# Two-layer kernel: softmax division moved behind the weighted values, and the values' projection by seven half-size products

## The chip, the core and the metric

The kernel runs on one core of a Trainium2 chip. The metric is the device time of one execution in microseconds (us). Times of single instructions come from one profiled execution. The core's engines run side by side, each through its own queue in order: TensorE (PE; PEld is its weight load), VectorE (DVE), ScalarE (ACT), GpSimd (POOL) and SyncE (SP), which here only issues DMA transfers. Matrix products land in eight PSUM banks of 128 partitions x 512 floats.

## The reference

The input x is 8 batch elements of 512 tokens of 256 channels, float32. Two layers follow one another; layer 1 of the change's title is the first. It normalises x, and adds causal attention with 16 heads of 64 channels (with biases and rotary embedding) and an int8-quantised linear map:

```python
xn = layernorm(x)
q, k, v = xn @ Wq + bq, xn @ Wk + bk, xn @ Wv + bv      # 1024 columns: 16 heads of 64
q, k = rope(q), rope(k)
scores = where(causal, q @ k.T / sqrt(64), -1e9)
attended = softmax(scores) @ v                            # per head
x = x + (attended @ Wo + bo) + quantised_linear(xn)
```

The second layer normalises again and adds a gated comparison softmax and a token-mixing feed-forward block. The change touches nothing in it.

## The kernel before

**Steps.** The first layer is worked through in 16 steps, called `at`: step `at = 2b + g` is half g (8 heads) of batch element b. A step's order is written out by hand in the loop `for at in range(1, last)` (`last` is 15); steps 0 and 15 are written out before and behind it. Each engine's queue takes its instructions in the order in which the functions are called.

**Projections.** `project_qk(n, which)` (L428, L434) projects q (`which` 0) or k (1) of four heads: two halves of two matmuls 128x512, each evicted from PSUM by ACT with its bias into `l`; then four DMAs (L436) put `l` with its partitions exchanged into `y`. `turn_qk` does the rotary embedding: on DVE `h = l*cos` (`turn_own`, L446) and `y = y*sin` (`turn_other`, L446), on POOL `h = h + y` (L461). Step `at` uses the heads of projections `2at` and `2at+1`; they are made one step earlier. `project_v(at)` (L472, L478, L479) makes the values of the next step with eight matmuls of 128x512 columns; ACT evicts them, a DMA stores them to HBM, and `load_v` (L489) brings them back with their partitions in another order. A matmul in float32 is two records in the profile.

**Scores.** `scores(at, run)` (L509) computes, for five runs of query blocks of 32, the scores of all heads side by side on the array. `soften` follows each run: DVE adds the mask and finds the row maximum (L537), and ACT takes the exponential and sums it (L541). `divide` takes the reciprocal of the sums on DVE (L552) and multiplies every probability by it on POOL (L560; in step 0 some on ACT, L558). `turn` transposes 32x32 blocks on DVE (L580). `weigh` (L597) multiplies with the values on TensorE, `keep_weighed` (L611) evicts four banks on ACT and adds the values' bias. `finish` is the output product with Wo (`output_product`, L390) and its addition to x on DVE (`add_output`, L399), which frees the product's bank.

**The input.** `look_at` takes the statistics of a batch element and lets POOL raise them to the power -1/2 (L158); `prepare` normalises it on DVE (L172) and finds its greatest magnitude (L306). `turn_x` transposes it on DVE into a tile `xs` (L325), stores it (`xnf`, L329) and loads it back as `xnT` (L188), which the projections read. In the last steps `fetch_input` also loads the first elements' normalised input again as `xnl`, which shares its tile with `xs`; `round_input` (L192), `clip` (L197, L201) and `add_quantised` (L209 to L218) do the quantised map.

**Order of a step before.** In the words of the functions: scores(at, 0), turn(at-1, 4), soften; weigh(at-1), keep_weighed(at-1); rotary of the next keys; scores 1, soften, turn 0, divide; `project(at+1, 0)`, the next queries; scores 2, soften, rotary, turn 1; turn_x in even steps; `project_v(at+1)`; scores 3 and 4 with their soften, turn and divide; `finish(at-1)`; `project(at+2, 1)`, the keys of the step after the next. Tiles of PSUM come from a ring of eight banks: a new tile waits until the one eight tiles earlier has been read.

Of the kernel before, what the change touches and what calls it, by code (L numbers as in the profile page):

```python
# [16 lines left out]
P = 128  # L17
B, S, D = 8, 512, 256
H, L = 16, 64
NT = S // P  # L20
# [14 lines left out]
PLACE = {i: n for n, i in enumerate(i for us in UNITS for i in us)}  # L35
# [9 lines left out]
def two_layers(  # L45
# [214 lines left out]
    with ExitStack() as c0:  # L260
# [120 lines left out]

        products = {}

        def output_product(at, half):

            pw = bank(f"pw_{at}_{half}").rearrange("p (j n) -> p j n", j=2)
            for j in range(2):
                tok = bass.ts(2 * half + j, P)
                for p in range(4):
                    nc.tensor.matmul(  # L390
                        pw[:, j, :], atts[at, p][:, tok], wo[:, 4 * (at % NH) + p, :],
                        start=(p == 0), stop=(p == 3),
                    )
            products[at, half] = pw
# [20 lines left out]
        def project_qk(at, which):  # L415


            b, g = divmod(at, NG)
            w = wqkv[which]

            l, y = (
                prob.tile([P, 2, S], F32, tag="p", name=f"{tag}_{at}_{which}") if at == 1 else
                work.tile([P, 2, S], F32, tag=tag, name=f"{tag}_{at}_{which}", bufs=2) for tag in "ly"
            )
            for t in range(2):
                pb = bank(f"pq_{at}_{which}_{t}")
                for k in range(NK):
                    nc.tensor.matmul(  # L428
                        pb.rearrange("p (t a r) -> p t a r", a=4, r=Q), w[:, g, k, bass.ts(t, P)],
                        xnT[b][:, k].rearrange("p a (t r) -> p t a r", r=Q),  # L430
                        start=(k == 0), stop=(k == NK - 1),
                    )
                bias = BIAS + which * NP + 2 * g + t
                nc.scalar.activation(l[:, t, :], pb, AF.Identity, bias=cs[:, bias : bias + 1])  # L434
            for n in range(4):
                nc.sync.dma_start(y[bass.ts(n ^ 1, Q)], l[bass.ts(n, Q)])  # L436
            evicted[at, which] = l, y
# [45 lines left out]

        def load_v(at):

            there = stores.pop(at)
            vs[at] = work.tile([P, 4, NT, P], F32, tag="vr", name=f"vr_{at}")
            for j in range(4):
                nc.sync.dma_start(  # L489
                    vs[at][j * Q : j * Q + Q].rearrange("p c t n -> p c (t n)"),  # L490
                    there[j].rearrange("(c k) n -> k c n", c=4),
                )
# [23 lines left out]
        def soften(at, run):  # L516

            if at not in sums_of:
                sums_of[at] = [
                    small.tile([P, 2 * len(PLACE)], F32, tag=f"{n}16", name=f"{n}_{at}", bufs=2)  # L520
                    for n in ("nm", "sm", "rs")
                ]
            nm, sm, _ = sums_of[at]
            for us in RUNS[run]:
# [7 lines left out]
                for i in us:  # L532
                    n = Q * (i + 1)
                    chances[at, i] = p[:, :, col : col + n]
                    for e, sc in enumerate(scored.pop((at, i))):
                        c = 2 * PLACE[i] + e
                        nc.vector.tensor_tensor_reduce(  # L537
                            p[:, e, col : col + n], sc, cmask[:, S - n :], -1.0 / L**0.5, BIG,
                            ALU.add, ALU.min, nm[:, c : c + 1],
                        )  # L540
                        nc.scalar.activation(  # L541
                            p[:, e, col : col + n], p[:, e, col : col + n], AF.Exp,
                            bias=nm[:, c : c + 1], scale=-1.0, accum_out=sm[:, c : c + 1],
                        )
                    col += n

        def divide(at, run, on_act=False):
            _, sm, rs = sums_of[at]
            for us in RUNS[run]:
                first = 2 * PLACE[us[0]]  # L550
                which = slice(first, first + 2 * len(us))
                nc.vector.reciprocal(rs[:, which], sm[:, which])  # L552
                for i in us:
                    for e in range(2):
                        c = 2 * PLACE[i] + e
                        p = chances[at, i][:, e, :]
                        if on_act and us is RUNS[run][-1]:
                            nc.scalar.activation(p, p, AF.Copy, scale=rs[:, c : c + 1])  # L558
                        else:
                            nc.gpsimd.tensor_scalar(p, p, rs[:, c : c + 1], 1.0, ALU.mult, ALU.mult)  # L560

# [4 lines left out]
        def turn(at, run):  # L568
# [6 lines left out]
            for i in (i for us in RUNS[run] for i in us):  # L575
# [29 lines left out]
        def keep_weighed(at):  # L605
            g = at % NH
            for j, av in enumerate(weighed.pop(at)):
                atts[at, j] = attp.tile([P, S], F32, tag="att", name=f"att_{at}_{j}")

                bv = BIAS + 2 * NP + 4 * g + j  # L610
                nc.scalar.activation(atts[at, j], av, AF.Identity, bias=cs[:, bv : bv + 1])  # L611
# [200 lines left out]
        divide(0, 0)  # L812
# [4 lines left out]
        divide(0, 1, on_act=True)  # L817
# [8 lines left out]
        divide(0, 2)  # L826
# [9 lines left out]
        divide(0, 3, on_act=True)  # L836
        divide(0, 4)
# [4 lines left out]
        for at in range(1, last):  # L842
# [5 lines left out]
            turn(at - 1, 4)  # L848
# [15 lines left out]
            divide(at, 0)  # L864
            turn_qk(2 * at + 3, 1)
            if at == last - 2:
                first_norm = norm(0, xpool.tile([P, NT, D], F32, tag="x", name="yn_0"))
# [8 lines left out]
            elif g == 1 and 1 <= b < B - 2:  # L876
                look_at(b + 2)
            divide(at, 1)
            if at == last - 1:
                first_norm()  # L880
            project(at + 1, 0)
            if at in (last - 3, last - 2):
# [8 lines left out]
            divide(at, 2)  # L891
            if at == 2:
                prepare(2)
            elif g == 1 and 1 <= b < B - 2:
                prepare(b + 2)
            if g == 0 and 1 < b < B - 1:
                turn_x(b + 1)
                if b + 2 < B:
                    x_next.append(load_x(b + 2))
            if at == last - 1:  # L900
                turn_qk(2 * at + 3, 0)
            if at == 1:
                nc.gpsimd.tensor_tensor(bob, bob, rw[:, 2, :], ALU.add)
                add_biases(0)
            project_v(at + 1)
            if at == last - 1:
                break
            if at == 2:
# [3 lines left out]
            soften(at, 3)  # L912
            turn_qk(2 * at + 3, 0)
            turn(at, 2)
            divide(at, 3)
            scores(at, 4)
            soften(at, 4)
# [3 lines left out]
            finish(at - 1)  # L921
            turn(at, 3)
            if two:
                project(at + 2, 1)
            divide(at, 4)
# [11 lines left out]
        divide(at - 1, 3)  # L937
# [6 lines left out]
        divide(at - 1, 4)  # L944
# [5 lines left out]
        turn(at - 1, 4)  # L950
        add_output(at - 2, 1)
        fetch(B - 1)
        divide(at, 0)
# [6 lines left out]
        divide(at, 1)  # L960
        keep_weighed(at - 1)
        load_v(at)
# [7 lines left out]
        divide(at, 2)  # L970
# [5 lines left out]
        divide(at, 3)  # L976
# [5 lines left out]
        divide(at, 4)  # L982
        kk = key(0)
        turn(at, 4)
        r = gate(0)
# [124 lines left out]
```

## Time and profile before

| What | Value |
|---|---|
| Time, median of 3 runs | 935.56 us (935.55 to 936.3) |
| Profiled execution: span from first to last instruction | 934.3 us; its own time outside the trace is not listed apart, the runs lie 1.3 us above the span |
| PE busy | 919.8 us (98%) |
| PEld, DVE, ACT, POOL busy | 594.7, 793.3, 528.3, 542.2 us |
| Granted TensorE clock | 1.000 |
| First layer's steps on the chain (starts of scores 0, steps 2 to 14) | 115.93, 163.36, 207.59, 253.73, 297.96, 342.94, 387.18, 431.68, 475.92, 521.62, 565.85, 612.07, 657.00 us |
| L472, values' projection | 256 records of 128x512, 114.3 us |
| L390, output product | 512 records of 128x256, 114.9 us |
| L560, divides on POOL | 504, 265.4 us |
| L552, reciprocals on DVE | 144, 15.7 us |
| DMA | 108.03 MB, 116 GB/s over the span |

The page's group rows give an engine, an operation, its output and inputs by the program's names, the shape, the count, and then busy time, mean ns of one, and the idle time of the engine just before, with what ended it. The chain that ended last is followed back from the last instruction, at each step to what released it.

### The profile page before, as it was taken

How to read it: one execution, taken by the hardware profiler on the slowest of the kernel's cores; microseconds unless marked ns; L12 is line 12 of the kernel's file. 1: busy time of each engine (PE TensorE's matmuls, PEld its weight loads, DVE VectorE, ACT ScalarE, POOL GpSimd, SP SyncE). 2: the span in 40 equal slices, each digit the busy share in tenths (PEclk: the TensorE clock that was granted, in tenths of full speed). 3: DMA queues.
4: the chain of work that ended last, by engine and by line, in shares of the span. 5: the costliest groups of instructions: out<-in, count | busy, mean ns of one | idle time of the engine just before them, and what ended most of it. 6: DMA issues, size and time to landing. Idle time of an engine off the chain costs nothing.

```text
span 934.3 us, 27432 instructions
## 1 busy us (share of the span) xinstructions
PE 919.8 (98%) x10451; PEld 594.7 (64%) x10451; DVE 793.3 (85%) x2441; ACT 528.3 (57%) x1478; POOL 542.2 (58%) x688
## 2 busy tenths in 40 slices
PE   9998999999999999999999999999999999999998
PEld 5446565656566575757565656566657777777776
DVE  4998898898899889988998899999899588888854
ACT  3585564647465646474746556555577444445553
POOL 2576766655665667566665756678667323444311
PEclk9999999999999999999999999999999999999999
DMA  7667354525543464245444635563435133221011
GB/s 213 194 165 213 102 138 130 121 75 132 169 105 97 109 182 132 75 115 172 123 95 114 179 93 145 151 154 97 110 108 127 47 102 79 74 50 48 25 33 34
DMA packets 70290, 108.03 MB, mean 116 GB/s; under 512 B 8592, under 2 KB 49040, under 8 KB 70160
## 3 DMA queue, kind: packets, MB, share of 16 engines
q1 hardware_dynamic: 68288, 104.64, 42.2%
q10 hardware_dynamic: 1872, 1.64, 0.7%
q8 instruction: 83, 1.36, 0.6%
q14 instruction: 47, 0.39, 0.1%
HBM read 41.76 MB, written 28.84 MB: 76 GB/s over the span
## 4 chain that ended last, share of the span: by engine, by line
PE 85%; DVE 6%; DMA 3%; issue 1%; POOL 1%; SPq 1%; ACT 1%; DVEq 0%; ACTq 0%; POOLq 0%
PE pq L428 21%; PE av L597 14%; PE sc L509 11%; PE pw L390 10%; PE pv L472 8%; PE po L756 6%; PE pk L703 3%; PE pg L718 3%; PE pvv L730 3%; DVE t L580 2%; PE c L675 2%; PE trc L743 1%; PE plr L245 1%; DVE p L537 1%; DMA xnl<-xnf 1%
## 5 line engine op out<-in xcount | busy, mean ns | idle before, releaser
L541 ACT ACTIVATE p<-p,nm 128x64 f32<-128x64 f32 (+15 forms) x512 | 260.0, 512 | 123.8 <-DVE nm L537 100.9
L560 POOL TENSOR_SCALAR p<-p,rs 128x512 f32<-128x512 f32 (+4 forms) x504 | 265.4, 547 | 44.6 <-DVE rs L552 42.6
L461 POOL TENSOR_TENSOR h<-h,y 128x1024 f32<-128x1024 f32 x62 | 161.1, 2598 | 181.5 <-DVE y L446 102.2
L537 DVE CUSTOM_DVE_ANT_0 p<-sc,cmask 128x64 f32<-128x64 f32 (+15 forms) x512 | 190.2, 434 | 53.7 <-PE sc L509 53.7
L580 DVE STREAM_TRANSPOSE t<-p 128x256 f32<-128x256 f32 (+3 forms) x640 | 192.2, 367 | 17.9 <-POOL p L560 17.8
L509 PE MATMUL sc<-h,h 64*32 64x512 f32 (+15 forms) x4096 | 138.7, 393 | 1.3 <-POOL h L461 1.2
L597 PE MATMUL av<-t,vr 32*64 32x384 f32 (+15 forms) x4096 | 128.8, 392 | 3.7 <-issue 3.7
L597 PEld LDWEIGHTS av<-t,vr 32*64 32x64 f32 x4096 | 122.8, 131 | 9.2 <-issue 7.9
L509 PEld LDWEIGHTS sc<-h,h 64*32 64x32 f32 x4096 | 78.6, 106 | 78.5 <-issue 58.3
L434 ACT ACTIVATE l<-pq,cs 128x512 f32<-128x512 f32 x128 | 84.7, 683 | 67.6 <-PE pq L428 53.3
L390 PE MATMUL pw<-wo,att 128*128 128x256 f32 x512 | 114.9, 382 | 0.8 <-DVE nm L537 0.8
L446 DVE TENSOR_TENSOR y<-y,cs 128x1024 f32<-128x1024 f32 x64 | 110.6, 1728 | 5.1 <-DMA y<-l 5.1
L428 PE MATMUL pq<-xnT,wq 128*128 128x512 f32 x256 | 114.6, 599 | 0.2 <-ACT xnT L349 0.2
L428 PE MATMUL pq<-xnT,wk 128*128 128x512 f32 x256 | 113.1, 593 | 1.4 <-DVE x L399 1.0
L472 PE MATMUL pv<-wv,xnT 128*128 128x512 f32 x256 | 114.3, 599 | 0.0
L390 PEld LDWEIGHTS pw<-wo,att 128*128 128x128 f32 x512 | 95.9, 190 | 19.5 <-issue 6.1
L541 ACT ACTIVATION_READ_ACCUMULATOR p<-p,nm 128x1 f32 x512 | 97.3, 190 | 0.0
L428 PEld LDWEIGHTS pq<-xnT,wk 128*128 128x128 f32 x256 | 48.3, 190 | 58.2 <-issue 55.4
L472 PEld LDWEIGHTS pv<-wv,xnT 128*128 128x128 f32 x256 | 47.3, 190 | 57.9 <-issue 54.5
L446 DVE TENSOR_TENSOR h<-l,cs 128x1024 f32<-128x1024 f32 x64 | 80.0, 1252 | 4.3 <-ACT l L434 4.3
L428 PEld LDWEIGHTS pq<-xnT,wq 128*128 128x128 f32 x256 | 47.2, 190 | 56.0 <-issue 48.8
L611 ACT ACTIVATE att<-av,cs 128x512 f32<-128x512 f32 x64 | 38.7, 688 | 71.3 <-PE av L597 71.3
(114 smaller groups left out, 940.7 us busy)
## 6 DMA issues: line engine op xcount, KB each, us to landing
y<-l SPq DMA_DIRECT2D x256, 128.0 KB, 2.3
va<-v SPq DMA_DIRECT2D x32, 512.0 KB, 3.1
vr<-va SPq DMA_DIRECT2D x64, 256.0 KB, 5.1
x<-in_x SPq DMA_DIRECT2D x15, 512.0 KB, 5.0
x1f<-x SPq DMA_DIRECT2D x7, 512.0 KB, 3.2
out<-y SPq DMA_DIRECT2D x14, 256.0 KB, 2.2
xnf<-xs SPq DMA_DIRECT2D x5, 512.0 KB, 3.6
xnT<-xnf SPq DMA_DIRECT2D x20, 128.0 KB, 2.8
```

Of the source, the lines that this page charges most:

```text
L390: nc.tensor.matmul(pw[:, j, :], atts[at, p][:, tok], wo[:, 4 * (at % NH) + p, :], start=(p == 0), stop=(p == 3),)
L428: nc.tensor.matmul(pb.rearrange("p (t a r) -> p t a r", a=4, r=Q), w[:, g, k, bass.ts(t, P)], xnT[b][:, k].rearrange("p a (t r) -> p t a r ...
L434: nc.scalar.activation(l[:, t, :], pb, AF.Identity, bias=cs[:, bias : bias + 1])
L446: nc.vector.tensor_tensor(dst, src, table[:, None, :].to_broadcast([P, 2, S]), ALU.mult)
L461: (engine or nc.gpsimd).tensor_tensor(h, h, y, ALU.add)
L472: nc.tensor.matmul(pb.rearrange("p (g n) -> p g n", g=2), xnT[b][:, k, 2 * half + j], wqkv[2][:, 2 * g : 2 * g + 2, k, :], start=(k == 0), ...
L509: nc.tensor.matmul(scored[at, i][e][j * Q : j * Q + Q, :], q[rows, j % 2, bass.ts(i, Q)], k[rows, j % 2, :n], start=True, stop=True,)
L537: nc.vector.tensor_tensor_reduce(p[:, e, col : col + n], sc, cmask[:, S - n :], -1.0 / L**0.5, BIG, ALU.add, ALU.min, nm[:, c : c + 1],)
L541: nc.scalar.activation(p[:, e, col : col + n], p[:, e, col : col + n], AF.Exp, bias=nm[:, c : c + 1], scale=-1.0, accum_out=sm[:, c : c + 1],)
L560: nc.gpsimd.tensor_scalar(p, p, rs[:, c : c + 1], 1.0, ALU.mult, ALU.mult)
L580: nc.vector.transpose(turned[at][c][:, :, at_ : at_ + (n - 1) * pitch(c) + 1 : pitch(c), :], p[:, :, c * P : c * P + n * Q].rearrange("p e ...
L597: nc.tensor.matmul(banks[j][e * L : e * L + L, i * Q :], vs[at][rows, c, m, bass.ts(e, L)], t[c][rows, e, m * pitch(c) + m : m * pitch(c) ...
```

## The change

Three things are changed, and the hand-written order of a step with them.

First, `divide` is gone. `weigh` works on the exponentials; `settle` takes the reciprocals of all sums of a step at once, transposes them on DVE, writes them to HBM and loads them back spread over the partitions (`share`), and `share_out` multiplies the weighted values by them on POOL (in step 15 two of four on DVE). The values' bias no longer goes through `keep_weighed`: since probabilities sum to one, `gather_bias` and `spread_bias` put its product with Wo once into the output's bias row. `soften` is split into `lower` (DVE) and `raise_` (ACT).

Second, in steps 1 to 14 `project_v(at+1)` is replaced by `project_v_by_seven(at+1)`: seven products of half the size in place of eight (Winograd's form), with differences of the input's quarters made on POOL (`mix_input`, once per batch element), sums of the weights made once on POOL (`sum_weights`), and the results put together by accumulation in PSUM, four ACT copies and three DVE additions. Its products stand among the halves of the keys' projections; in step 14 they stand alone.

Third, moved: `finish(at-1)` from the end of the step to the place where `project_v` stood; `turn_x` of steps 4, 6, 8, 10 in front of the queries' projection, and `look_at` and `prepare` in odd steps to an earlier place; `turn_x` of step 12 stays behind `clip`; the rotary embedding of the step's last queries goes behind `lower(at, 4)`.

```diff
+        def mix_input(b):
+            t = work.tile([P, 4, 2, P], F32, tag="tx", name=f"tx_{b}")
+            (b11, b12), (b21, b22) = ([xnT[b][:, k, 2 * h : 2 * h + 2] for h in range(2)] for k in range(NK))
+            for dst, x, y in ((0, b12, b11), (1, b22, t[:, 0]), (2, b22, b12), (3, b21, t[:, 1])):
+                nc.gpsimd.tensor_tensor(t[:, dst], x, y, ALU.subtract)
...
+        def project_v_by_seven(at, amid={}):
...
+            x, y, z = (bank(f"pv_{at}_{n}").rearrange("p (j n) -> p j n", j=2) for n in range(3))
...
+            product(x, b11, a11, True)
+            keep(0, 0)
+            then(0)
+            product(y, b21, a12, True)
+            product(z, t1, s1, True)
+            product(x, t2, s2)
+            keep(1, 0)
+            add(y, 0, 0)
+            then(1)
+            product(x, t3, s3)
+            keep(1, 1)
+            then(2)
+            add(z, 1, 1)
+            product(x, t4, a22)
+            keep(0, 1)
+            store(0)
+            then(3)
+            product(z, b22, s4)
+            add(z, 1, 0)
+            store(1)
...
-        def divide(at, run, on_act=False):
...
+        def settle(at):
+            sm = sums_of.pop(at)[1]
...
+            nc.vector.reciprocal(rs, sm)
+            nc.vector.transpose(turned_, rs)
+            there = away.tile([4, 2, S], F32, tag="rs", name=f"rsf_{at}")
+            nc.sync.dma_start(there.rearrange("j e (i q) -> (j e i) q", q=Q), turned_)
+            shares[at] = work.tile([P, 4, S], F32, tag="share", name=f"share_{at}")
+            for e in range(2):
+                nc.sync.dma_start(
+                    shares[at][e * L : e * L + L], there[:, e, :][None].to_broadcast([L, 4, S])
+                )
...
+        def share_out(at, j):
+            nc.gpsimd.tensor_tensor(atts[at, j], atts[at, j], shares[at][:, j, :], ALU.mult)
...
             scores(at, 0)
-            turn(at - 1, 4)
+            if at == 1:
+                turn(at - 1, 4)
+                settle(at - 1)
             soften(at, 0)
...
-            divide(at, 0)
             turn_qk(2 * at + 3, 1)
+            for j in range(4):
+                share_out(at - 1, j)
+            if g == 1 and 1 <= b < B - 2:
+                look_at(b + 2)
...
             elif g == 1 and 1 <= b < B - 2:
-                look_at(b + 2)
-            divide(at, 1)
+                prepare(b + 2)
+            if g == 0 and 1 < b < B - 2:
+                turn_x(b + 1)
+                x_next.append(load_x(b + 2))
...
             project(at + 1, 0)
+            if at == 1:
+                sum_weights()
+            if g == 1:
+                mix_input(b + 1)
...
-            divide(at, 2)
+            if at == last - 3:
+                turn_x(b + 1)
...
-            if g == 0 and 1 < b < B - 1:
-                turn_x(b + 1)
-                if b + 2 < B:
-                    x_next.append(load_x(b + 2))
...
-            project_v(at + 1)
             if at == last - 1:
+                project_v_by_seven(at + 1)
                 break
+            finish(at - 1)
...
             scores(at, 3)
-            soften(at, 3)
-            turn_qk(2 * at + 3, 0)
-            turn(at, 2)
-            divide(at, 3)
+            lower(at, 3)
+            raise_(at, 3)
             scores(at, 4)
-            soften(at, 4)
+            turn(at, 2)
+            lower(at, 4)
...
-            finish(at - 1)
-            turn(at, 3)
-            if two:
-                project(at + 2, 1)
-            divide(at, 4)
+            turn_own(2 * at + 3, 0)
+            turn_other(2 * at + 3, 0)
+            project_qk(2 * at + 4, 1)
+
+            def step_one():
+                raise_(at, 4)
+
+            def step_two():
+                turn(at, 3, slice(0, 1))
+                project_qk(2 * at + 5, 1, (0,))
+
+            def step_last():
+                turn(at, 3, slice(1, 2))
+                turn(at, 4)
+
+            project_v_by_seven(
+                at + 1,
+                {0: step_one, 1: step_two, 2: lambda: project_qk(2 * at + 5, 1, (1,)), 3: step_last},
+            )
+            settle(at)
```

## The prediction

> **What bounds the kernel now.** I read the page first (busy time, then the costliest groups), then the chain of work that ended last in order of time, then the timelines of VectorE, GpSimd and the SyncE queue over the steps on which the change acts.
>
> ```profile
> PE 919.8 (98%) x10451; PEld 594.7 (64%) x10451; DVE 793.3 (85%) x2441; ACT 528.3 (57%) x1478; POOL 542.2 (58%) x688
> ```
> ```profile
> 431.68 1.89 PE sc L509 x45
> 433.57 7.95 PE av L597 x163
> 441.51 2.05 PE sc L509 x56
> 443.56 7.06 PE pq L428 x16
> 450.62 1.94 PE sc L509 x64
> 452.56 7.06 PE pv L472 x16
> 459.63 2.32 PE sc L509 x80
> 461.95 7.10 PE pw L390 x32
> 469.05 6.87 PE pq L428 x16
> 475.92 1.89 PE sc L509 x45
> ```
> The second fence is step 9 (at=9) on the chain, start and length in us. Its nine pieces are all TensorE and sum to 44.24: TensorE is the bound, with no gap. The starts of "sc" give every step's length: steps 3, 5, 7, 9, 11 take 44.2 each; steps 4, 6, 8, 10 take 46.1, 45.0, 44.5, 45.7; step 12 46.2; step 13 44.9. So removed TensorE work is paid out in time, unless something else then comes late. What is nearly late:
>
> ```profile
> 441.50:486.50 45.00, 44.66 (x593) 27.60 (x592) 41.91 (x138) 26.17 (x80) 28.27 (x38) 1.00 0.43 107
> ```
> ```profile
> PE pq L428 <- DVE x L399: 1.0, 1, 1.0
> ```
> ```profile
> 504.84 1.20 DVE xs L325 x2
> ...
> 506.06 3.93 DMA xnf<-xs
> ...
> 511.30 3.07 DMA xnT<-xnf
> 514.37 0.14 issue
> ```
> From step 9 into step 10 (first line, a stretch: length, then PE, PEld, DVE, ACT, POOL) VectorE is busy 41.9 of 45.0. The second, from the waits, shows TensorE once held by the add of the output product, which frees a PSUM bank. The third, from the chain of step 10, is an input's way through HBM: from the end of `xs`, 506.04, to landed `xnT`, 514.37, 8.3 us.
>
> **The products.** Now a step has 16 records of 128x512 (L472), 7.06 us. Then 14 matmuls of 256 columns, 28 records; L390 has 32 such records in 7.10, so 28 take 6.21. Saved 0.85 in each of 14 steps, 11.9 us. An undisturbed step would take 43.4 us. In it, counted from its first score, the pieces would start at: weigh 1.9, scores 9.8, q projection 11.9, scores 18.9, output product 20.9, scores 28.0, keys' first half (2at+4) 30.3, seven products with the other keys' halves 33.8 to 43.4.
>
> **Divides, beginning.** POOL loses 504 divides (265.4 us), DVE 144 reciprocals (15.7). In the steps these lie under TensorE; in the beginning they don't: TensorE is busy 39.3 of 42.0 us between 40 and 82, with 2.3 us of wait before the first weigh (72.5), where the transposes follow divides. Without them I take −2.3 (from 0 to −2.7, the whole idle time). A step gains on DVE three adds from PSUM (L399: 0.68 each) and a reciprocal and transpose (0.25 by L552 and L580), and loses nine reciprocals (1.0 to 1.3): net +1.0. POOL gains four share-outs of 128x512 (L735: 1.27 each, 5.1) and in odd steps four differences of 128x256 (L380: 0.73 each, 2.9).
>
> **The shares' round trip.** A write of 16 KB and two reads of 512 KB per step: 2.3 (y<-l) and 5.1 (vr<-va), so 7 to 10 us after `settle`. They must be there when POOL has done its two `h` adds, 12.9 into the next step. The DMA share in 437.8 to 442.4 is 0.02, so the engines are free then: nothing, up to 2 us a step if it lands late.
>
> **Even steps 4, 6, 8, 10: a queue is passed.** `turn_x` moves ahead of the q projection, so on SP its store, four loads and the next x load now stand before the eight y<-l of q; SP waits there for the store to land. `xs` can't end before 17.7 (scores of run 1 softened by 13.7 as at 445.4 in step 9; nine transposes 2.7; xs 1.2). In step 8 SP was through with these DMAs 5.3 us after xs (416.6 to 421.9), in step 10 6.2; four y<-l at 0.55 and a landing of 2.3 make y late at 27 to 28. DVE's y product then ends at 28 to 29, turn(1) (2.8) at 31 to 32, and only then comes the add (0.65) that frees the bank of the keys' first half: 31.5 to 32.6 against 30.3. The late exponentials then hold ACT's copy of the first product by 0.6. In all 1.8 to 2.9 a step; I take 2.2. Before, these steps were 4.5 over four times 44.2, in part because xnT came late.
>
> **Odd steps 3 to 11: DVE is full.** Its work ahead of that same add: soften 2.7, the four rotary products 6.8 (the last takes 3.38, POOL's `h` add standing at its side), statistics 1.8, soften 2.75, transposes 2.7, normalise 2 and maximum 1.15, soften 2.75, rotary 2.3, transposes 2.8, add 0.65. From 1.1 that sums to 29.5; but the normalise waits for POOL's power, which stands behind the four share-outs (17.9+1.0=18.9, against 17.7): 30.5 to 31.3. And it then runs beside the four differences on POOL:
>
> ```profile
> 437.88 3.35 POOL L461 TENSOR_TENSOR h<-h,y 128x1024 f32<-128x1024 f32 x1 [4.92 <-DVE rs L552]
> ```
> ```profile
> 438.93 3.38 DVE L446 TENSOR_TENSOR y<-y,cs 128x1024 f32<-128x1024 f32 x1
> ```
> Alone these take 2.36 and 1.22; side by side both are stretched. For a tensor_scalar beside a POOL tensor_tensor the nearest rows are L197 and L201 next to L708: 2.13 for the two against 1.07. So 0 to 1 more. Stall per odd step with ACT's 0.6: 0.8 to 2; I take 1.3.
>
> [...]
>
> **Steps 3 to 11 together:** before 402.4 (the nine lengths). After 9×43.4 + 4×2.2 + 5×1.3 = 405.9: +3.5.
>
> **Step 12: the wait that was hidden.** Here xs shares a tile with the fetched xnl and comes after `clip`, as before (end 596.83, 31.0 into the step; its y landed at 590.5). xnT landed 7.1 to 8.3 later: at 38 to 39. Before, the keys' projection that reads it began at 605.2, 39.4 in: covered. Now the output product stands earlier and the keys' first half would start at 31.2 (0.85 for the quantised product included), in front of the products that could have covered the landing. Stall 7 to 8: 43.4+0.85+7.5=51.7 against 46.2, +5.5. [...]
>
> **Step 14 and the turn to layer 2.** Here the seven products stand without keys between them. Copy, product, copy go in turn: the first copy waits for ACT's exponentials (24.7), and the last product for a DVE add behind two rotary pairs and a transpose run (31.5), so scores(14,3) start at 32.4 instead of 27.9: +4.5. What followed had a stall of its own (1.2 at 691, and the divides ahead of it) that the longer time absorbs; scores(15,0) end 2.2 later than before. I take +2.3. The last settle's landing lies under the 7.8 us of weigh, and share-out under value and compare (5.6): nothing.
>
> **Steps 1, 2, 13:** −0.85; −0.85 and +0.45 for spread_bias; −0.85 and about +0.7 of the copies' wait: −1.4 together.
>
> **Sum** on the profiled span of 934.3: −2.3 + 3.5 + 5.5 + 2.3 − 1.4 = +7.6, so 941.9. The runs' median of 935.56 is 1.3 above the span: 943.2; I say 942.
>
> **Rivals.** (a) Faster: VectorE and the y loads keep up, steps 3 to 11 fall to 43.4 to 43.9 each. For it: in even steps DVE is busy only 37.8 of 44.5, and the order in which products and keys alternate leaves each copy about 2 us. Against: y behind the x loads is an order, not a matter of load. Sum −2.3 −9 (9×43.7=393.3 against 402.4) +5.5+2.3−1.4: 930.5; with step 14 free as well 927. Chance 0.36. It decides if the bank's add in steps 4 to 11 ends before 30.3. (b) My forecast, slower, 937.5 to 948: 0.50. (c) Slower still, a share-out that waits for its shares or a normalise held 2.9: POOL's chain becomes late and with it the output product at 20.9, 1 to 1.5 more in nine steps, 951 to 955: 0.08. (d) No change, the stalls just eating the 11.9: within 1.9 us of 935.6: 0.06. Differences under 0.2% (1.9 us) can't be told from none here. That the products aren't shortened at all can be left out: 28 records of 256 columns are what the program issues.
>
> Faster 0.36, same 0.06, slower 0.58. The range, 926 to 951, takes in the faster case down to its free step 14 and leaves out most of (c).
>
> **What would show it.** Right: pv of about 6.2 us a step; idle time on the keys' L428 records released by DVE's add (2.2 in even steps, 1.3 in odd) and, in step 12 alone, 7 to 8 by DMA xnT<-xnf; a wait of DVE's y product for DMA y<-l in steps 4, 6, 8, 10; ACT's first copy holding the third x product. Wrong: steps 4 to 11 of 43.4 to 43.9 without waits, or a step 12 under 47.

## Result and profile after

| | before | after |
|---|---|---|
| Median | 935.9 us (935.55 to 936.3, 4 runs) | 1028.9 us (1024.1 to 1034.8, 4 runs) |
| Ratio | | 1.0995, interval 1.0956 to 1.1034 |
| Profiled execution, span | 934.3 us | 1027.2 us (of a run of 1028.98) |
| Granted TensorE clock, mean | 1.000 | 0.955 |
| DMA | 108.03 MB | 125.08 MB |
| Steps 3 to 11, starts of scores 0 | 402.5 us | 466.8 us |

The change costs 93 us. The page after, its first row and the row of the granted clock:

```profile
PE 940.7 (92%) x10621; PEld 636.3 (62%) x10621; DVE 833.2 (81%) x2374; ACT 520.0 (51%) x1468; POOL 399.8 (39%) x294
...
PEclk9999999898999898989999898979999999999999
```

TensorE still has the most work, and more than before although its products were cut; it also stands still for 8% of the span. What stood in the way, from the waits of TensorE, VectorE and GpSimd (total, times, longest):

```profile
DVE y L470 <- DMA y<-l: 52.8, 9, 9.9
PE pq L452 <- DVE x L420: 52.2, 10, 8.3
...
POOL att L731 <- DMA share<-rsf: 35.4, 13, 5.0
...
DVE x L171 <- POOL rstd_a L157: 20.3, 6, 4.9
```

The second line is the wait that the prediction named: the keys' first half waits for the output product's add, which frees its bank. It was 1.0 in all; now 3.8 to 8.3 in every step from 3 to 11. How the add becomes late stands on the chain, for step 7 (odd) and step 6 (even):

```profile
370.90 1.91 DMA y<-l
372.81 5.29 DMA rsf<-rt
378.81 7.20 DMA share<-rsf
386.17 4.98 POOL att L731 x4
392.17 3.10 DVE x L171 x4
404.92 6.30 PE pq L452 x8
```
```profile
336.15 5.16 DMA xnf<-xs
345.54 4.48 DMA y<-l
354.76 5.79 PE pq L452 x8
```

Odd: the shares' write lands behind the values' stores, the shares land 16.1 us into the step (it began at 369.95), the share-outs hold POOL, the statistics' power stands behind them, and the normalise, the transposes and the add follow. Even: q's swaps wait in SP's queue for the next input's store, and y lands 32.0 us into the step (318.04). In both, the eight records of the keys then take 5.8 to 6.3 instead of 3.7. A window on them (length, PE, PEld, DVE, ACT, POOL, granted clock, DMA share, GB/s):

```profile
354.80:358.20 3.40, 3.40 (x4) 1.47 (x5) 3.40 (x18) 2.39 (x9) 0.00 (x0) 0.50 0.38 154
358.20:361.60 3.40, 3.40 (x11) 2.00 (x10) 3.40 (x14) 3.08 (x11) 0.00 (x0) 0.88 0.00 0
```

The clock granted in the 3.4 us after the stall is 0.50, in the next 0.88. Where the 93 us lie, by step starts: start of step 1 −1.2; steps 1, 2 and 13 +7.6; 3 to 11 +64.3; 12 +12.0; 14 +5.1; step 15 and layer 2 +5.1.

### The profile page after: what moved, and what is told of

The parts are those of the page before. It is cut to its first block, busy times and chain, and to the rows that moved or that the text cites. A ratio compares the mean times of both kernels' runs of the same rounds, so it can differ in the third digit from the quotient of the medians.

```text
span 1027.2 us, 27478 instructions
## 1 busy us (share of the span) xinstructions
PE 940.7 (92%) x10621; PEld 636.3 (62%) x10621; DVE 833.2 (81%) x2374; ACT 520.0 (51%) x1468; POOL 399.8 (39%) x294
## 2 busy tenths in 40 slices
DMA packets 81298, 125.08 MB, mean 122 GB/s; under 512 B 11408, under 2 KB 51856, under 8 KB 81168
## 4 chain that ended last, share of the span: by engine, by line
PE 57%; DMA 16%; DVE 15%; POOL 5%; SPq 3%; issue 2%; ACT 1%; DVEq 0%; POOLq 0%
PE pq L452 14%; PE pv L541 7%; PE av L711 7%; PE po L876 5%; DVE t L694 4%; PE sc L613 4%; DVE p L645 4%; DMA share<-rsf 4%; DMA y<-l 3%; DMA rsf<-rt 3%; PE pw L412 3%; POOL att L731 3%; PE pk L823 3%; PE pg L838 3%; PE pvv L850 3%
## 5 line engine op out<-in xcount | busy, mean ns | idle before, releaser
L452 PE MATMUL pq<-xnT,wk 128*128 128x512 f32 x256 | 140.7, 693 | 56.8 <-DVE x L420 52.2
L711 PE MATMUL av<-t,vr 32*64 32x160 f32 (+15 forms) x4096 | 132.0, 393 | 3.1 <-issue 3.1
L452 PEld LDWEIGHTS pq<-xnT,wk 128*128 128x128 f32 x256 | 56.1, 225 | 120.6 <-DVE x L420 57.2
L412 PEld LDWEIGHTS pw<-wo,att 128*128 128x128 f32 x512 | 97.1, 192 | 22.2 <-issue 8.0
L731 POOL TENSOR_TENSOR att<-att,share 128x512 f32<-128x512 f32 x62 | 77.5, 1283 | 50.8 <-DMA share<-rsf 35.4
L726 ACT COPY att<-av 128x512 f32<-128x512 f32 x62 | 31.9, 601 | 78.8 <-PE av L711 78.8
L808 ACT ACTIVATE e<-c,nb 128x512 f32<-128x512 f32 x32 | 21.7, 684 | 74.8 <-DVE nb L803 74.2
L876 PE MATMUL po<-cut_t,ptc 128*128 128x256 f32 x224 | 49.5, 379 | 0.0
```

The lines of the kernel that those rows point to most:

```text
L412: nc.tensor.matmul(pw[:, j, :], atts[at, p][:, tok], wo[:, 4 * (at % NH) + p, :], start=(p == 0), stop=(p == 3),)
L452: nc.tensor.matmul(pb.rearrange("p (t a r) -> p t a r", a=4, r=Q), w[:, g, k, bass.ts(t, P)], xnT[b][:, k].rearrange("p a (t r) -> p t a r ...
L711: nc.tensor.matmul(banks[j][e * L : e * L + L, i * Q :], vs[at][rows, c, m, bass.ts(e, L)], t[c][rows, e, m * pitch(c) + m : m * pitch(c) ...
L731: nc.gpsimd.tensor_tensor(atts[at, j], atts[at, j], shares[at][:, j, :], ALU.mult)
L876: nc.tensor.matmul(po[:, j, :], pt[at // 2][:, j, m, :], xn[:, m, :], start=(m == 0), stop=(m == NT - 1),)
```

## Experiments

Theory T: the shares come late and hold the power behind them (odd steps). Theory Q: SP's queue holds q's swaps (even steps). Rivals: VectorE is overfull (F), the seven products cost (S). Below, the line numbers of the changed kernel hold where nothing else is said.

**The power ahead of the share-outs.**

```diff
+            if g == 1 and 1 <= b < B - 2:
+                look_at(b + 2)
             for j in range(4):
                 share_out(at - 1, j)
-            if g == 1 and 1 <= b < B - 2:
-                look_at(b + 2)
```

> In the odd steps 3 to 11 the statistics' power stands ahead of the four share-outs on GpSimd; nothing else differs. Theory T (the shares land some 17 us into the step, the power waits behind the share-outs, and so the normalise and the output product's add come late): VectorE's wait for the power (20.3 us in the profile after) goes, the stalls of the keys' first half in the odd steps fall from 3.8-4.9 to 0-1.5 and their eight records from 5.4-6.3 to near 3.5; five steps times about 5.3 is 26: 997 to 1009 us. Theory F (VectorE's own queue is overfull, so the add would be as late without that wait): within 5 us of 1029.

1016.3 us (1.0832, 1.0784 to 1.088). The wait for the power is gone, the odd steps fall from 49.7–51.4 to 46.0–46.7 and their stalls to 0.3–1.9 us, after which the eight records take 3.70. T holds in the odd steps. But the even steps became no shorter, step 12 rose from 58.2 to 63.2, and the whole gained 12.6 us, half of what T said.

**q's swaps from ScalarE's queue, steps 4, 6, 8, 10.**

```diff
-            project(at + 1, 0)
+            project(at + 1, 0, nc.scalar if g == 0 and 1 < b < B - 2 else None)
```

> In the even steps 4, 6, 8 and 10 the eight transfers that swap the rows of the q projection are issued from ScalarE's queue, behind its own copies, and no longer from SyncE's behind the next input's store, loads and the load of x. Theory Q (that queue makes y late in the even steps): VectorE's wait for y falls from up to 9.9 to under 3, the stalls of 6.0-8.3 to 0-2, the slow records with them; four steps times about 7.5 is 30: 992 to 1006 us. Theory F (VectorE overfull): within 5 us of 1029.

1000.6 us (1.0665, 1.0599 to 1.073). The even steps fall from 52.0–55.0 to 43.9–45.7; the odd ones stay at 48.9–51.6. Q holds. F falls as the cause of the large stalls; a small part of it comes back below.

**Both.**

> The two edits together. If T and Q each hold and act in different steps, the gains add: 965 to 985 us, with steps 3 to 11 near 44 to 46 each. If a third cause, VectorE's load, stands right behind: 985 to 1005. F: above 1015.

978.5 us (1.0429, 1.0386 to 1.0472). Steps 3 to 11 take 407.7 us: 59 of their 64 are gone. In those steps the wait for the bank is now

```profile
PE pq L452 <- DVE x L420: 7.2, 5, 2.3
```

where it was 51. Of the 41.9 us left over the kernel before (spans), steps 12 to 14 hold 26.1 and step 15 and layer 2 hold 8.3. In step 12 the queue is again the cause, by the chain of this run: q's swaps stand behind the loads of `xnl`.

```profile
588.25 14.63 DMA xnl<-xnf
...
604.82 2.65 DMA y<-l
...
619.49 5.12 PE pq L452 x8
```

**One trip instead of sixteen.** `settle` returns after step 0's shares, which all later steps use; their own shares are left out.

```diff
+            if at > 0:
+                shares[at] = shares[0]
+                return
             there = away.tile([4, 2, S], F32, tag="rs", name=f"rsf_{at}")
```

> The reciprocal sums are written out and read back as shares once, after step 0; all later steps multiply by these (left out: the later steps' own shares and their 15 round trips, 1.0 MB moved in each). Theory T: the odd steps recover as with the power moved ahead, 997 to 1009; if the trip's traffic also slows the values' and the input's transfers (8.8 and 6.0 us after, 5.1 and 3.6 before), the even steps gain too: 975 to 997. F: within 5 us of 1029.

985.1 us (1.05, 1.0458 to 1.0541): fifteen trips cost 44 us in this order, waits and traffic together. Odd steps 45.7, even 51 to 53: Q stays. What holds the odd steps at 45.7, 1.5 more than before, is VectorE's own load, here in step 7 (a stretch: length, then PE, PEld, DVE, ACT, POOL):

```profile
360.61:406.31 45.70, 43.88 (x605) 29.80 (x605) 44.77 (x134) 25.70 (x80) 19.16 (x13) 1.00 0.38 94
```

Its 44.8 us of work are more than the 43.4 that TensorE would need. So F holds in the odd steps, but for 1.5 us each. Below, all five odd steps take 45.7 again without the trips, and 43.1 to 44.4 in the first try for a faster kernel, which among other things moves the normalise to GpSimd (VectorE is then busy 41.3 of 43.7 in step 7).

**The seven products undone.** `project_v` in two halves where the seven stood; `mix_input` and `sum_weights` gone.

```diff
-            project_v_by_seven(
-                at + 1,
-                {0: step_one, 1: step_two, 2: lambda: project_qk(2 * at + 5, 1, (1,)), 3: step_last},
-            )
+            project_v(at + 1, (0,))
+            step_one()
+            step_two()
+            project_v(at + 1, (1,))
+            project_qk(2 * at + 5, 1, (1,))
+            step_last()
```

> The changed kernel with the values by their ordinary products again, in two halves between the keys' halves; the undivided probabilities, the shares and the order stay, the differences and sums for the seven products go. Theory T+Q (the order and the round trip cost the time): the stalls stay, the 0.85 us a step comes back and the three adds and the differences go: 1010 to 1040 us. Rival S (the seven products' adds and differences overfill VectorE and GpSimd): 955 to 985.

993.5 us (1.0601, 1.0558 to 1.0645), between the ranges of S and T+Q: without the seven products 35 of the 93 us are gone, so S holds in part. Steps 3 to 11 lose 33 of them, the odd ones 27. The even steps stay at 50.5 to 52.9 (Q), the odd steps fall to 44.4–46.1. Two of its rows show what became shorter, against the changed kernel's. The normalise (duration min/median/max in ns), after and here:

```profile
L171 DVE TENSOR_SCALAR x<-x,mv_a,rstd_a x20: 809/814/882, 187.8 to 606.4; 128x256 f32<-128x256 f32 x20
```
```profile
L171 DVE TENSOR_SCALAR x<-x,mv_a,rstd_a x20: 408/410/416, 183.8 to 574.1; 128x256 f32<-128x256 f32 x20
```

In the changed kernel the pieces of step 7 (from 392.17) stand beside POOL's four differences (392.11 to 395.10), and each takes twice its time. And the shares' write, on this run's chain (step 7 begins at 358.4), takes 1.84 where it took 5.29, since the values' stores no longer stand right ahead of it:

```profile
362.21 1.84 DMA rsf<-rt
...
364.75 7.69 DMA share<-rsf
```

**Settle earlier**, ahead of the stores.

```diff
             def step_two():
+                settle(at)
                 turn(at, 3, slice(0, 1))
```

> The changed kernel with settle (reciprocals, transpose, the write of 16 KB and the two reads of 512 KB) moved from the step's end, behind the values' stores, to ahead of the third unit's transposes, some 8 us earlier and ahead of those stores on SyncE's queue; nothing else differs. Theory T2 (the trip is late because it stands behind the seven products' late stores: its write took 5.3 us there and 1.9 where the ordinary products' stores came earlier): the shares land before GpSimd has made the keys' h adds, its waits for them (35.4 us) go, the odd steps recover as with the power moved ahead, and the even steps gain a little from the emptier queue: 990 to 1010 us. Rival (the trip's traffic delays other transfers wherever it stands): 1015 to 1030, with the values' or y's transfers later instead.

1006.6 us (1.0749, 1.0728 to 1.0771). Odd steps 45.7–48.2 with stalls under 0.9 at the keys, as T2 said. New are stops of 0.7 to 2.8 us in the middle of nearly every weigh, which the profile puts to "issue".

**The early settle and q's swaps from ScalarE together.**

> The early settle together with q's swaps of the even steps issued from ScalarE. T2 and Q as separate waits: steps 3 to 11 at 44 to 45.5 each, 965 to 980 us; what stays over the kernel before lies in steps 1, 12, 13, 14 and the turn to layer 2. If the odd steps keep over 1.5 us of stall each, VectorE's load is a third cause: 980 to 995.

976.2 us (1.0424, 1.0392 to 1.0456): no better than with the late settle. Steps 3 to 11 take 415.8, with at most 0.3 us of stall at the keys and stops of 1.4 to 2.4 us in most weighs. A third cause.

**A stall of chosen length in the kernel before.**

```diff
+            if at in DOSES:
+                for _ in range(DOSES[at]):
+                    nc.vector.tensor_copy(late_tile, cmask)
             finish(at - 1)
```

> The kernel before, unchanged in its arithmetic, with 8, 11, 14, 17 and 20 idle copies of a 128x512 tile put on VectorE ahead of the output product's adds in steps 3, 5, 7, 9 and 11, so that the keys' projection waits a chosen time for its bank. Theory G (the clock follows the stall): a stall under 1.9 us leaves the first eight records of the keys' projection at 3.7 us; stalls over 2.8 us stretch them to 5 to 6.6, as in the profile after. Rival (the slow records after belong to the changed kernel's data or order): they stay at 3.7 however long the stall.

977.8 us, one time. The stall came elsewhere than expected: the keys did not wait, but the next step's weigh did, behind VectorE's last transposes. The reading is the same (start, length, instruction, records, and the idle time before; L597 is the kernel before's weigh), steps 4, 6, 8 and 10:

```profile
214.58 9.48 PE L597 MATMUL av<-t,vr 32*64 32x512 f32 x256 [3.75 <-issue]
```
```profile
311.46 10.70 PE L597 MATMUL av<-t,vr 32*64 32x512 f32 x256 [5.14 <-issue]
```
```profile
409.21 9.69 PE L597 MATMUL av<-t,vr 32*64 32x512 f32 x256 [6.53 <-issue]
507.60 9.98 PE L597 MATMUL av<-t,vr 32*64 32x512 f32 x256 [7.90 <-issue]
```

A weigh takes 8.02 undisturbed. So stalls of 3.75, 5.14, 6.53 and 7.90 us cost 1.5, 2.7, 1.7 and 2.0 more behind them, in a kernel whose arithmetic is the old one: G holds, and the loss doesn't grow with the stall. In steps 3 to 11 of the other runs a stall of the keys up to 1.93 left their eight records at 3.7, 2.3 stretched them to 5.4, and from 2.9 on they took 5.1 to 6.8. Elsewhere, waits of 2.0 to 2.7 us did either: 1.99 was followed by sixteen records of 8.83 instead of 7.13 (version 4 below, step 1), 2.68 by an output product of the usual 7.14 (the seven products undone, step 1).

**Undivided probabilities alone, order of before** (loop of before, `settle` and `share_out` in it, ordinary products, bias by `gather_bias`).

> The kernel before in its own order with the undivided probabilities alone: settle after the last transposes of the step before, the share-outs on GpSimd behind the first h add of q, 14 us before the output product reads them; values by their ordinary products, the bias through the gathered row. Theory T+Q (the earlier output product is what the round trip is too slow for): the trip is hidden here, 928 to 938 us, the beginning 2 us shorter. Rival (the trip costs by its traffic wherever it stands, 1.0 MB a step on the same queue): 945 to 970.

975.4 us (1.041, 1.038 to 1.044), above both ranges. Here the share-outs stood behind q's `h` add and the output product waited for them, 9.2 us in all from 112 to 700 us; the odd steps took 45.5, and steps 1, 2 and 12 were 4 to 8 longer. Version 2 took these waits away; `settle` also moved from the next step's start to the end of its own:

```diff
             turn_qk(2 * at + 3, 1)
+            for j in range(4):
+                share_out(at - 1, j)
...
             turn_qk(2 * at + 2, 0)
-            for j in range(4):
-                share_out(at - 1, j)
...
             finish(at - 1)
+            settle(at)
```

> The kernel before in its own order with the undivided probabilities alone, settle now at the end of its own step and the share-outs behind the keys' h adds, so that neither waits for the other: nothing of the trip lies on a path. Theory T2: the odd steps return from 45.5 to 44.2, steps 1 and 12 lose their share-out waits: 935 to 955 us. Rival (its 1.0 MB a step costs by itself): 960 to 975, as in the first version.

977.5 us (1.0447, 1.0418 to 1.0475), no shorter, so T2 does not hold here. In steps 2 to 13 nearly all that is left is the stop in the weigh. The waits of steps 2 to 13 (112 to 700 us), before and here:

```profile
PE av L597 <- issue: 1.3, 4, 0.4
```
```profile
PE av L711 <- issue: 28.3, 14, 3.3
```

Those steps are 30.5 us longer than before; step 15 and layer 2 are 8.7 longer, again with stops of 3.2 and 1.8 us in weighs. Windows on the weigh of step 9, before and here, and on the stop:

```profile
431.60:439.50 7.90, 7.90 (x237) 6.80 (x244) 6.71 (x18) 4.18 (x13) 2.98 (x3) 1.00 0.43 96
```
```profile
447.40:455.30 7.90, 7.90 (x223) 6.50 (x223) 3.83 (x13) 4.17 (x13) 0.00 (x0) 1.00 0.91 231
455.30:458.60 3.30, 0.08 (x2) 0.00 (x0) 2.21 (x2) 0.00 (x0) 0.86 (x1) 1.00 0.33 82
```

The DMA share ahead of the stop is 0.91 against 0.43: theory I, the trip's traffic itself stops TensorE. Four runs test it.

**Like traffic on the kernel before**, to nobody's use:

```diff
+            for half in range(2):
+                nc.sync.dma_start(
+                    idle[2 * half : 2 * half + 2, :, 0, :].rearrange("t p n -> (t p) n"),
+                    x[half].rearrange("(r t) c -> r (t c)", t=2),
+                )
```

> The kernel before, with two idle copies of 512 KB in rows of 2 KB from HBM to HBM issued on SyncE at the start of each of the 14 steps; nobody waits for their data. Theory I (traffic of this size during the weigh stops TensorE, which then waits for its own code): stops of 1 to 3 us in the middle of the weighs that the profile gives no releaser for, where the kernel before has 1.3 us in all from step 2 on; 950 to 975 us. Rival (the stops belong to the undivided probabilities): weighs of 7.9 as before, 936 to 942.

956.8 us (1.0197, 1.0172 to 1.0223). The arithmetic of before, and the stops are there, in the weigh (L597) and in the scores behind it (L509):

```profile
PE sc L509 <- issue: 7.4, 5, 2.1
...
PE av L597 <- issue: 5.7, 7, 1.3
```

**The undivided kernel (version 2) without the later trips**, and so without the later steps' own shares.

> The undivided probabilities in the order of before, with the shares of step 0 kept for all later steps but the tail's (left out: the later steps' own shares, 15 round trips). Theory I: the stops in the weighs go (28.3 us in steps 2 to 13 with the trips), 926 to 938 us. Rival (TensorE stops for something else in the undivided form): 955 to 975, with the stops still there.

933.8 us (0.995, 0.9933 to 0.9967): no stop is left, and step 2 starts 4.3 us earlier than before. So the form itself costs nothing and gains some 4 us; the trips cost 44 us in this order too.

**The trip moved away from the weigh.** `read_shares` is the two reads, taken out of `settle`. Version 3 puts them behind q's swaps, and the output product behind the keys:

```diff
             project(at + 1, 0)
+            if at > 1:
+                read_shares(at - 1)
...
-            finish(at - 1)
...
                 project(at + 2, 1)
+            finish(at - 1)
```

> The undivided probabilities in the order of before, the shares' two reads issued behind q's swaps, some 22 us into the step, so that they run beside projections and not beside the weigh; the share-outs behind q's first h add and the output product behind the next keys' projection, so that neither is late. Theory I: the weighs are whole again and the projections, with 16 matmuls of 512 columns where the weigh has 256 small ones, are not stopped: 928 to 942 us. If any traffic of this size stops TensorE wherever it stands: 955 to 975.

985.6 us (1.0503, 1.0479 to 1.0527): odd steps 44.1–44.5 with whole weighs, but even steps 52.9–54.8, since the keys moved ahead of the output product now waited for the input (`xnT`) 5.8 to 7.7 us: the wait that the prediction saw for step 12, in five steps. Version 4 keeps the order:

```diff
             load_v(at)
+            if at > 1:
+                read_shares(at - 1)
```

> The undivided probabilities in the order of before, the trip's write at the step's end, its two reads behind the values' loads (issued at the end of the weigh, so that they run beside q's projection), the share-outs on GpSimd behind the power and ahead of q's h add, the output product where it was. Theory I: weighs and keys without stops, odd steps 44.2, even 44.4 to 46; 928 to 940 us, at or a little under the kernel before. If the amount of traffic counts wherever it stands: 950 to 975.

973.2 us (1.0382, 1.0364 to 1.0401). Nearly whole weighs and odd steps of 44.1–44.2; in the even steps the reads now delay y (5.9 instead of 2.3 us in step 6) and y the transposes, for which the weigh waits 0.5 to 1.6; `xnT` comes late behind them, and the keys wait 0.9 to 3.4; steps 12 and 13 wait 3.1 and 4.0 for `xnl`. Both versions miss theory I's range: the long stops in the weigh are gone, but the same traffic makes other transfers late.

**The changed kernel with early settle and q's swaps from ScalarE, without the later trips**, and so without the later steps' own shares.

> The changed kernel with the early settle and q's swaps from ScalarE, and the shares of step 0 kept for all later steps (left out as above). Theory I: the stops in the weighs go, steps 3 to 11 from 45.7 to 43.4-44.2 each, the whole from 976 to 945-958 us, the rest over the kernel before being steps 12 to 14. Rival: unchanged stops, 970 to 980.

956.6 us (1.0199, 1.0165 to 1.0233), 20 less than with the trips. Steps 3 to 11: 409.1; odd 45.7 with 1.0–1.5 of stall at the bank; step 12 still 53.2.

**What ends the stops.** The profile names no releaser, but the traces hold every DMA packet, those of the two queues of kind "instruction" too. On the first of these, q8, packets of 16 KB run, one to 253 TensorE instructions in the profile after (84 packets; 10621 matmuls and as many weight loads): I read them as TensorE's code. In the stop of step 9 above there is one:

```profile
q1 hardware_dynamic: 100, 0.25, 29.4%
q8 instruction: 1, 0.02, 2.2%
```

It ran from 455.89 to 457.08, and TensorE went on at 458.69. All 18 stops of over 0.4 us inside a weigh or a group of scores of this run that the profile puts to "issue", and all 12 under the idle traffic, end 1.2 to 1.7 us after such a packet has landed; so do all 125 of the twenty profiles. Without the later trips version 2 has none. By that reading the stops are waits for TensorE's own code; what is measured is the interval behind the packet.

**Towards a faster kernel.** None of three tries is faster. The first moved everything at once (normalise on GpSimd, input turned early, output product late):

> Undivided probabilities and seven products, with each wait found so far moved: the output product behind the last scores, its adds behind the last softening; the power and the differences ahead of the share-outs, the normalise on GpSimd behind them; the input turned at the start of the even steps, step 12's too; q's swaps of steps 12 and 13 from ScalarE; step 14's products between scores and the output product; the output weights loaded at the start of step 1. If waits alone made the change slower, steps 3 to 11 take 43.4 to 44.5 each and the whole 920 to 940 us. If VectorE's load or the clock keeps them late: 945 to 975.

1016.0 us (1.0841, 1.0796 to 1.0886). Odd steps took 43.1 to 44.4, four of five under the 44.2 of before: there the seven products pay. Even steps took 51.8–55.8: the input's loads, moved, now ran beside the shares and the values, and VectorE waited up to 10.1 us for y.

The second is the early settle with q's swaps from ScalarE, the output weights loaded earlier and step 14's order changed:

> The early settle and q's swaps from ScalarE, and further the output weights loaded at the start of step 1, and step 14's seven products with the output product's first half ahead of them and the scores of run 3 and the second half between them. Against the version without these two: step 14 back from 48 to 43.6, step 1 shorter by 2: 958 to 972 us. If step 1 or the turn to layer 2 is held by something else: 970 to 980.

981.0 us (1.0475, 1.0449 to 1.0502). Step 14 fell from 49.4 to 45.2, but the weigh behind it waited 2.1 us and took 10.3 instead of 8.4, and step 1 became longer (53.5).

The third leaves all steps as before but step 0:

> The kernel before with step 0 alone undivided: its nine groups of divides go, one settle and one trip in step 1 (into the values' tile, the values of step 1 loaded behind the share-outs), four share-outs on GpSimd ahead of the second group of divides, the values' bias added on VectorE; all other steps as before. Theory I (each trip is a cost, the divides cost only where nothing covers them, in step 0): step 2 starts 2 to 4.5 us earlier, 931 to 934 us. Rival (one trip and the extra operations in step 1 eat the gain): 935 to 940.

941.8 us (1.0047, 1.0032 to 1.0063). The four share-outs took 6.9 us on POOL from 90.0 on, ahead of step 1's divides; these came late, the output product waited 5.0, and step 2 started at 119.7 instead of 115.9. No complete kernel here beats the one before.

## Why the prediction was wrong

- **Sign and place: right.** The change is slower, and the wait is the one forecast: keys' first half, freed by the output product's add; y late in even steps, VectorE and the power late in odd ones. The sizes were not: of the sum −2.3 + 3.5 + 5.5 + 2.3 − 1.4 the profile shows −1.2, +64.3, +12.0, +10.2 and +7.6. Over the undisturbed 43.4, the five odd steps lost 36.2 us instead of 6.5, the four even ones 40.0 instead of 8.8.
- **The 407.7 us with both waits moved are no confirmation of the 405.9.** That figure holds 15.3 us of waits, which were moved; without them the sum would be 390.6. The undisturbed 43.4 left out VectorE's own 44.8 us of work in an odd step and the stops in the weigh.
- **The shares' round trip: the term that failed in the odd steps.** "7 to 10 us after `settle`", nothing to 2 a step. In step 7 it began 2.9 us into the step, behind the stores, and took 13.2 from the write's start to landing (372.81 to 386.01): the write 5.3 (taken: 2.3), the reads 7.2 (5.1). The DMA share of 0.02 that justified it was that of before; the seven products' stores, moved to the step's end, now stood there. The stall was 3.8–4.9 instead of 1.3. Without 15 of the 16 trips the kernel takes 44 us less. And a trip costs by its traffic too, which the forecast put at nothing: 20 us in the order with the early settle, 44 in the order of before.
- **The power behind the share-outs** was seen, and timed at 18.9 us into the step by shares that come in time; in step 7 it ended 22.2 in (392.14).
- **Normalise beside POOL's differences.** Taken 0 to 1 more; measured 1.6 (4 pieces of 0.81 instead of 0.41). No run shows rival (c)'s normalise held for 2.9, the length of the four differences.
- **Even steps.** Queue seen, prices too low: y at "27 to 28", measured 32.0 in step 6, since the store took 5.2 (3.9 in the quoted row of before) and y 4.5 (2.3). Stall 6.0–8.3 instead of 2.2.
- **The clock: a term left out.** The sum has nothing for slower records behind a stall. With the stalls 2.7 to 3.8 times as long as forecast, the keys' records of steps 3 to 11 took 52.4 instead of 33.3, 19.1 us in all, 1.4 to 2.6 a step; in step 6 the granted clock was 0.50 in the 3.4 us behind a stall of 6.03. In the runs above a stall of 2.9 was already followed by 6.66 us for the eight records, and 2.0 to 2.7 by slower ones sometimes.
- **Step 12**: +12.0 instead of +5.5, and not by `xnT` alone: in the profile after, the quantised product waits 5.7 for the output product's add, then the keys 4.5.
- **Step 14 and the turn**: +10.2 instead of +2.3. `scores(14, 3)` start 34.9 us into the step, not 32.4: the products wait 2.5, 0.7 and 0.7 for ACT's copies. The absorption came about in part: the stall of 1.2 is gone, and `scores(15, 0)` end 5.1 later, 1.9 less than that start is late. What was put at nothing is the +5.1 behind: two stops, 2.3 us in scores and 1.4 in a weigh, with slower records after them. Without the later trips that stretch is 0.6 longer than before.
- **Steps 1, 2 and 13**: +7.6 instead of −1.4. In step 1 the output product, now earlier, waits 3.9 for its weights (`wo`) and takes 8.8 instead of 7.1; in step 13 the quantised product waits 2.8 for the output product's add.
- **Rival (c)** named the late shares, at 0.08, and priced them through the output product. They acted through the power behind them on GpSimd. (a) and (d) fall: no step became shorter than before. The range ended 78 us below the result: the errors (transfer prices, what stands behind, clock, traffic) push the same way, and the bounds had added none of them to another.

What stays open: why TensorE's code, if that is what the packets bring, comes late. Its packets take no longer than before (median 1.15 us in version 2 and in the kernel before), so by that reading they start late; that they queue behind the trip's packets is my guess, not shown. What version 2 shows is stops of up to 3.3 us beside 1 MB of traffic a step.

## What to carry to other kernels

A transfer's price read in a calm stretch did not hold where the change itself had moved other transfers (the write: 2.3 us taken, 5.3 measured): go through what each queue holds at that moment, by the new order. Ask of a late operand not only who reads it but what stands behind the reader on its engine. And when removed arithmetic is bought with traffic, price the traffic against everything that shares the DMA engines; here 1 MB a step cost 44 us and most of the removed divides had been hidden.

## What the hardware showed

- With 1 MB a step of traffic that nothing reads, from HBM to HBM, the kernel before took 19.4 us (2.0%) longer, with stops of TensorE of up to 2.1 us in scores and 1.3 in weighs.
- All 125 stops of over 0.4 us of this kind in the twenty profiles ended 1.2 to 1.7 us after a 16 KB packet of q8, a queue of kind "instruction", had landed.
- Stalls of TensorE of 3.75 to 7.90 us before a weigh were followed by 1.5 to 2.7 us more in it. Behind the first of them the granted clock was 0.57 for 3.4 us and 0.93 for the next 3.4; in the changed kernel, behind 4.53 and 6.03, it was 0.50 for 3.4 us.
- A 16 KB write took 5.29 us where it was issued right behind 1 MB of stores (the changed kernel, step 7) and 1.84 where these were issued earlier (the seven products undone).
